# A linear-attention layer gated by an FP4 network: x1 is transposed by DMA in 16-bit halves in 23 of 32 blocks, and the first layer norm's gain and shift move to VectorE

## The chip, the core and the metric

The kernel runs on one core of a Trainium2 chip. The time is the device time of one execution in microseconds (us); each figure is a median of several runs. Engines are named as in the profile: PE is TensorE's matmul, PEld its weight load, DVE is VectorE, ACT is ScalarE, POOL is GpSimd, SP is SyncE, whose queue issues nearly all DMAs.

## What is computed

The input `x` is 4 x 2048 x 256 in float32. It is normalised once, and two branches use the result:

```python
xn = layernorm(x)                                   # no gain, no shift
# branch 1: linear attention with 16 heads of 64, then a feed-forward network
Q = elu(xn @ Wq + bq) + 1;  K = elu(xn @ Wk + bk) + 1;  v = xn @ Wv + bv
KV = einsum("bshd,bshm->bhdm", K, v)
Z = 1 / (einsum("bshd,bhd->bsh", Q, K.sum(1)) + 1e-6)
o = einsum("bshd,bhdm,bsh->bshm", Q, KV, Z)
x1 = layernorm(xn + o @ Wo + bo) * g1 + be1
s = layernorm(x1 + gelu(x1 @ W1 + b1) @ W2 + b2) * g2 + be2
# branch 2: a gated network on FP4-rounded activations and weights
g = silu(fp4_linear(silu(fp4_linear(xn, w_gate)) * fp4_linear(xn, w_up), w_down))
out = x + s * g
```

The change concerns the line of `x1`, and how its result reaches the product with `W1`, which needs it transposed.

## The kernel before

A batch has 2048 tokens and is cut into eight blocks of 256, so there are 32 blocks, n = 0 to 31. A block lies on chip as 128 partitions of two tokens (index `j`) by 256 features.

A prologue prepares the weights and sums the keys of the first batch. Then the loop over n runs the query side of block n: Q, the attention product, the first layer norm, the feed-forward network and the FP4 network, spread in a software pipeline over neighbouring iterations. In the first three batches the same iterations also work off the keys of the next batch ("subs", two per block): in the first four blocks of a batch's turn the keys' inputs are normalised and transposed (`f == 0`), in the last four they are loaded back from memory for the other half of the heads. The last batch, blocks 24 to 31, has no keys beside it.

All of TensorE's instructions keep the order in which the program writes them (`mm` and `tr`, lines 102 to 106; the profile gives their lines as L103 and L106). For the other engines and for SP's queue a planner orders the instructions ahead of time, by the program's order and by what it expects to be ready; `tc.issue_after(ins)` puts instructions behind a given one on its engine. Once ordered, each engine takes its list strictly in turn and waits at the head of it.

Around the change an iteration n runs thus (lines 1221 to 1285):

- `attention_norm(n)` (line 951): mean and variance of x1 on VectorE, the power -1/2 on GpSimd (line 430), then two `tensor_scalar` on VectorE give (x1 - mean) * rstd. Gain and shift are not applied here.
- `keys_in` for the next two subs; then on TensorE `ffn_2(n - 1, 20)`, the first 20 products of the second feed-forward matrix of the block before (`py`).
- `scales_h`, `scales_x`: VectorE finds the FP4 scales of the next blocks.
- `x1_T(n)` (line 956): four PE transposes of x1 into PSUM (`pt_x`), and two ScalarE activations that take them out into `x1T`, with g1 as scale and be1 as bias, each a column per feature.
- `keys_apart` (line 502) for both next subs. Where the keys' input was just normalised, it is transposed by DMA: ScalarE copies the upper and the lower 16-bit halves of the floats apart, one transposing DMA on SP moves both, and later `keys_T` (line 523) joins the halves by one ScalarE copy.
- `spread_scales`: a PE transpose of the scales (`pscale`), a store, and eight loads that spread them into `qT`.
- `ffn_2(n - 1, 28)`, then `q_of(n + 1)`: 32 matmul instructions (`pq`) in four PSUM tiles; each tile takes an exponential on ScalarE (`e`) and one VectorE instruction (`zq`).
- `grid_of_h`, `grid_T`, `grid_of_x` (FP4 rounding and its transposing DMAs), `output(n - 1)`, `keys_T` of the first next sub, and `ffn_1(n)` (line 968): 32 matmul instructions (`pf`) that read `x1T`, and gelu.

The joining copy of the second sub follows in the next iteration, behind the exponential of the first sub's keys. The tokens' own x1, wanted again in `output`, gets its gain and its shift on GpSimd in `ffn_addend` (line 811): times g1, plus a row `shift` that holds be1 + b2 (folded once by `add_b2`, line 267).

Buffers that matter: `mm_tile`, four PSUM banks in a ring for most products; tag `e` (three tiles: the exponentials of Q and of keys, and the keys' separated halves), tag `kk` (three: K's tiles and the transposed halves), and tag `zs` (one tile of three parts: sums that the attention product of the first three batches reads).

Of the kernel before, what the change touches and what calls it, by code (L numbers as in the profile page):

```python
# [8 lines left out]
F32 = mybir.dt.float32  # L9
# [13 lines left out]
def linear_attention_gated_by_fp4_ffn(  # L23
# [81 lines left out]
    def tr(*args, **kw):  # L105
        return tc.keep_in_program_order(nc.tensor.transpose(*args, **kw))  # L106
# [75 lines left out]
    for _ in range(24):  # L182
# [13 lines left out]
    W2_OF = {"11": 0, "21": 1, "22": 2, "t1": 3, "t2": 4, "t3": 5, "t4": 6}  # L196
    row_tiles = {
        name: const.tile([P, 1, D], F32, name=f"{name}_r")
        for name in ("bo", "g1", "shift", "g2", "be2")
    }  # L200
    rows = {name: t.to_broadcast([P, TB, D]) for name, t in row_tiles.items()}

# [3 lines left out]
    def load_row(name, v, dep):  # L206
        load_when(dep, row_tiles[name][:, 0, :], as_rows(v))
# [10 lines left out]
    def w2_sums():  # L218
# [20 lines left out]
            lambda dep: wv_bias(1),  # L239
            lambda dep: load_wv(0, dep),  # L240
            lambda dep: load_row("g1", g1, dep),
            lambda dep: load_row("shift", be1, dep),
            lambda dep: load_row("g2", g2, dep),
            lambda dep: load_row("be2", be2, dep),
        ],
# [18 lines left out]

    cols = {}

    def add_b2(dep):
        b2_r = work.tile([P, D], F32, tag="s", name="b2_r", bufs=1)
        load_when(dep, b2_r, as_rows(b2))
        shift = row_tiles["shift"][:, 0, :]  # L270
        nc.gpsimd.tensor_tensor(shift, shift, b2_r, ALU.add)

    def small_constants():


        vs = (("b1", b1), ("g1", g1), ("be1", be1))
        n = sum(v.shape[0] // P for _, v in vs)
        brow = work.tile([n, P], F32, tag="z", name="brow", bufs=1)
        r = 0
        for name, v in vs:  # L280
            k = v.shape[0] // P
            nc.sync.dma_start(brow[r : r + k, :], v.rearrange("(c p) -> c p", p=P))
            cols[name] = (r, r + k)
            r += k
        yield
        pb = mm_tile("pb")
        tr(pb[:, :n], brow, ident[:n, :n])
        bcol = const.tile([P, n], F32, name="bcol")
        vector.tensor_copy(bcol, pb[:, :n])
        for name, (lo, hi) in cols.items():  # L290
            cols[name] = bcol[:, lo:hi]
        yield


# [2 lines left out]
    def fp4_scale(x, am, name):  # L297

        nb = x.shape[1]
        rs = small.tile([P, I // BLK], F32, tag="rs", name=f"rs_{name}")[:, :nb]  # L300
        vector.tensor_reduce(am, x, AX.X, ALU.max, apply_absolute_value=True)
        vector.tensor_scalar(am, am, -1.0 / 6.0, -1e-12, ALU.mult, ALU.min)
        vector.reciprocal(rs, am)
        return rs
# [146 lines left out]

    xn_d, xnT_d = {}, {}
    keys = {}

# [42 lines left out]
            nc.sync.dma_start(xn, xn_d[n])  # L499
            nc.sync.dma_start(xnT, xnT_d[n])  # L500

    def keys_apart(b, sub, issue=None):
# [7 lines left out]
        half = keys[b, sub][0].bitcast(U16).rearrange("p j (c f h) -> p h c j f", c=ND, h=2)  # L510
        apart = work.tile([P, 2, ND, TB, P], U16, tag="e", name=f"apart_{n}", bufs=3)
        with tc.issue_after(issue) if issue is not None else nullcontext():
            for h in range(2):
                scalar.copy(apart[:, h], half[:, h])
        apartT = work.tile([P, 2, ND * T], U16, tag="kk", name=f"apartT_{n}", bufs=3)
        nc.sync.dma_start(
            apartT.rearrange("p h (m t) -> p (h m) t", t=P),
            apart.rearrange("p h c j f -> p (h c j f)"),
            transpose=True,
        )  # L520
        keys[b, sub].append(apartT)

    def keys_T(b, sub, issue=None):

        f, bi = divmod(sub, NB)
        if f > 0:
            return
        n = b * NB + bi
        xn, *apartT = keys[b, sub]
        xnT = work.tile([P, ND, T], F32, tag="xnT_k", name=f"xnT_k_0_{n}", bufs=3)  # L530
        if apartT:
            with tc.issue_after(issue):
                scalar.copy(
                    xnT.bitcast(U16).rearrange("p c (t h) -> p h (c t)", h=2), apartT[0]
                )
# [275 lines left out]
    def ffn_addend(n, behind=True):  # L811

        x1 = blk[n]["x1"]
        with tc.issue_after(pool["last"]) if behind else nullcontext():
            nc.gpsimd.tensor_tensor(x1, x1, rows["g1"], ALU.mult)
            pool["last"] = nc.gpsimd.tensor_tensor(x1, x1, rows["shift"], ALU.add).ins


    def q_of(n, chunks=range(NH)):
# [131 lines left out]
    def attention_norm(n):  # L951
        x1 = blk[n]["x1"]
        mv, rstd = stats(x1, f"1_{n}")
        normalize(x1, x1, mv, rstd)

    def x1_T(n):
        x1 = blk[n]["x1"]
        pt = transposes(x1, f"x1_{n}")
        x1T = work.tile([P, ND, T], F32, tag="x1T", name=f"x1T_{n}", bufs=1)
        for c in range(ND):  # L960
            ins = scalar.activation(
                x1T[:, c, :], pt[:, c, :], AF.Identity,
                bias=cols["be1"][:, c : c + 1], scale=cols["g1"][:, c : c + 1],
            )
        blk[n]["x1T"] = x1T
        blk[n]["act"] = ins.ins

    def ffn_1(n, chunks=range(NF)):
        x1T = blk[n]["x1T"]
# [80 lines left out]
    for n in range(NB):  # L1050
# [47 lines left out]
        ready = weight  # L1098
        if n == 4:
            w_down_sb = load_down()  # L1100
        if n == 5:
            add_b2(dep)
        if n == 6:
            load_xn(0)
            scales_x(0)
# [49 lines left out]
    for n in range(NBLK):  # L1155
# [80 lines left out]
        if more[0]:  # L1236
            scales_h(n + 1, 0)
            with tc.issue_after(qz_ins) if not subs else nullcontext():
                scales_h(n + 1, 1)
            if more[1]:  # L1240
                scales_x(n + 2)
        for sub in next_subs if n == 0 else ():
            keys_in(bn + 1, sub)
        x1_T(n)
        if not subs:
            ffn_addend(n, False)
        if n == last:
            gate_addend(n)
        for sub in next_subs:
            keys_apart(bn + 1, sub, blk[n]["act"])  # L1250

        if n > 0 and not subs:
            ffn_2(n - 1, 26)
# [2 lines left out]
        if n > 0:  # L1256
            ffn_2(n - 1, 28)
        if more[0]:
            q_of(n + 1)
        if more[0]:  # L1260
            grid_of_h(n + 1, 0)
            grid_T(n + 1, 0, NI)
# [9 lines left out]
            step(m_half)  # L1272
        for sub in next_subs[:1]:
            keys_T(bn + 1, sub, blk[n + 1]["exp"])
        if n + 1 == last:
            ffn_1(n, range(2))
            sums(last)
            ffn_1(n, range(2, NF))
            gpsimd_behind(blk[n]["hT"][:, NF - 1, :])
            gate_addend(n)  # L1280

            w2_last = wk_sb.rearrange("p c (e d) -> p (c e) d", d=D)
            nc.sync.dma_start(w2_last, by_chunks(W2))
        else:
            ffn_1(n)
# [46 lines left out]
```

## Time and profile before

| | us |
|---|---|
| median of 3 runs (1883.41 to 1885.26) | 1884.52 |
| the profiled execution | 1883.6 |
| its span on the core | 1881.8 |
| PE busy in it | 1860.8 |
| DVE busy in it | 1381.8 |
| ACT busy in it | 706.5 |
| POOL busy in it | 382.5 |

The span is the time between the first and the last instruction that the profiler saw; the execution's time also holds what lies around it. The rows of the instruction groups that the change touches, by the groups view (count, us busy in all, mean ns of one):

| engine, group | count | us | ns |
|---|---|---|---|
| PE, transposes of x1 (`pt_x`) | 128 | 21.5 | 282 |
| ACT, x1T out of PSUM, 128 x 256 | 64 | 32.6 | 560 |
| DVE, normalising x1, 128 x 256 | 64 | 23.5 | 410 |
| POOL, x1 times g1, 128 x 512 | 32 | 40.5 | 1266 |
| POOL, x1 plus shift, 128 x 512 | 32 | 41.4 | 1293 |
| ACT, keys' halves apart, 128 x 512 of 16 bits | 44 | 24.9 | 616 |
| ACT, keys' halves joined, 128 x 1024 of 16 bits | 22 | 29.4 | 1336 |

Matmul instructions overlap, so the sum of their durations is more than the time they take up: in the chain of waits the four transposes of a block take 0.44 us. How to read it: PE is busy in 99% of the span, and the 40 slices show a granted clock of full speed throughout. The other engines have free time, but within an iteration it is unevenly spread, so what matters for them is whether TensorE comes to wait for what they deliver.

### The profile page before, as it was taken

How to read it: one execution, taken by the hardware profiler on the slowest of the kernel's cores; microseconds unless marked ns; L12 is line 12 of the kernel's file. 1: busy time of each engine (PE TensorE's matmuls, PEld its weight loads, DVE VectorE, ACT ScalarE, POOL GpSimd, SP SyncE). 2: the span in 40 equal slices, each digit the busy share in tenths (PEclk: the TensorE clock that was granted, in tenths of full speed). 3: DMA queues.
4: the chain of work that ended last, by engine and by line, in shares of the span. 5: the costliest groups of instructions: out<-in, count | busy, mean ns of one | idle time of the engine just before them, and what ended most of it. 6: DMA issues, size and time to landing. Idle time of an engine off the chain costs nothing.

```text
span 1881.8 us, 25202 instructions
## 1 busy us (share of the span) xinstructions
PE 1860.8 (99%) x9324; PEld 1382.2 (73%) x9324; DVE 1381.8 (73%) x2524; ACT 706.5 (38%) x1190; POOL 382.5 (20%) x363
## 2 busy tenths in 40 slices
PE   8999999999999999999999999999999999999998
PEld 4456677777777777777777787777777788888887
DVE  5676677766677877777677787776776777888875
ACT  2343544324334335443233543353323333333332
POOL 1411322011122212220112221222101122222212
PEclk9999999999999999999999999999999999999999
DMA  5525655444535456635344654564443444444542
GB/s 182 194 77 127 116 120 102 100 102 94 96 63 99 111 98 122 143 66 110 81 89 79 119 100 104 94 139 90 91 88 71 104 77 83 89 83 84 92 83 50
DMA packets 229433, 188.77 MB, mean 100 GB/s; under 512 B 107687, under 2 KB 191155, under 8 KB 229310
## 3 DMA queue, kind: packets, MB, share of 16 engines
q1 hardware_dynamic: 228476, 185.58, 47.4%
q8 instruction: 74, 1.21, 0.3%
q10 hardware_dynamic: 834, 1.58, 0.3%
q14 instruction: 49, 0.40, 0.1%
HBM read 131.96 MB, written 32.59 MB: 87 GB/s over the span
## 4 chain that ended last, share of the span: by engine, by line
PE 77%; DVE 10%; DMA 9%; SPq 1%; issue 1%; POOL 1%; ACT 1%; POOLq 0%; DVEq 0%; ACTq 0%
PE pg L103 14%; PE pk L103 10%; PE pxk L103 10%; PE pf L103 9%; PE pa L103 8%; PE pq L103 8%; PE pd L103 7%; PE py L103 7%; DMA zb<-z_d 2%; DMA qT<-scale_d 2%; PE pz L103 1%; DMA xn_d<-xn_k 1%; DMA z_d<-z 1%; DVE x L119 1%; POOL rstd L430 1%
## 5 line engine op out<-in xcount | busy, mean ns | idle before, releaser
L430 POOL TENSOR_TENSOR rstd<-rstd,neg_half 128x2 f32<-128x2 f32 (+1 forms) x97 | 77.3, 797 | 1324.8 <-DVE rstd L119 964.9
L103 PE MATMUL pg<-wgu,qT 128*128 128x352 f32 x1024 | 308.5, 459 | 0.2 <-PE pm L103 0.2
L103 PEld LDWEIGHTS pg<-wgu,qT 128*128 128x128 f32 x1024 | 194.3, 190 | 113.8 <-issue 11.5
L103 PE MATMUL pk<-wk_sb,xnT_k 128*128 128x512 f32 x512 | 230.4, 592 | 1.2 <-ACT xnT_k L119 1.2
L103 PE MATMUL pf<-x1T,w_sb 128*128 128x256 f32 x1024 | 227.7, 380 | 2.2 <-DVE zq L119 1.6
L103 PE MATMUL pxk<-kk,xn_k 128*128 128x512 f32 x496 | 227.9, 598 | 1.1 <-DVE kk L119 1.1
L103 PE MATMUL pq<-xnT,wq_sb 128*128 128x256 f32 x1024 | 227.6, 380 | 0.9 <-DVE zq L119 0.8
L103 PEld LDWEIGHTS pf<-x1T,w_sb 128*128 128x128 f32 x1024 | 193.6, 190 | 32.3 <-DVE zq L119 6.0
L103 PEld LDWEIGHTS pq<-xnT,wq_sb 128*128 128x128 f32 x1024 | 191.8, 190 | 27.1 <-DVE zq L119 2.4
L119 DVE SCALAR_TENSOR_TENSOR kk<-ek,pk 128x512 f32<-128x512 f32 x128 | 85.5, 684 | 170.3 <-ACT ek L119 170.3
L103 PE MATMUL pd<-wd,qT 128*128 128x256 f32 x768 | 172.9, 380 | 1.1 <-DVE qT L119 1.1
L119 ACT ACT_TABLE_LOAD x121 | 155.2, 1283 | 49.2 <-PE pk L103 34.3
L103 PEld LDWEIGHTS pk<-wk_sb,xnT_k 128*128 128x128 f32 x512 | 97.0, 190 | 102.6 <-issue 90.3
L119 ACT ACTIVATE x1T<-pt_x,bcol 128x256 f32<-128x256 f32 x64 | 32.6, 560 | 357.8 <-PE pt_x L106 357.8
L103 PEld LDWEIGHTS pd<-wd,qT 128*128 128x128 f32 x768 | 145.3, 190 | 27.9 <-DVE qT L119 4.4
L103 PEld LDWEIGHTS pxk<-kk,xn_k 128*128 128x128 f32 x496 | 89.4, 190 | 99.2 <-issue 87.0
L119 DVE TENSOR_TENSOR h<-h,pg 128x352 f32<-128x352 f32 x128 | 66.0, 516 | 105.4 <-PE pg L103 103.2
L119 ACT ACTIVATE h<-pg 128x352 f32<-128x352 f32 x128 | 58.8, 459 | 211.3 <-PE pg L103 211.2
L119 ACT ACTIVATE hT<-pf,bcol 128x256 f32<-128x256 f32 x256 | 105.7, 471 | 66.0 <-PE pf L103 65.6
L119 DVE TENSOR_TENSOR zq<-zq,zb 128x1024 f32<-128x1024 f32 x64 | 79.2, 1238 | 64.9 <-DMA zb<-z_d 64.5
L103 PE MATMUL py<-w_sb,hs 128*128 128x128 f32 x992 | 122.0, 275 | 0.0
L119 ACT ACTIVATE e<-pq,neg_one 128x512 f32<-128x512 f32 x128 | 86.6, 685 | 84.7 <-PE pq L103 70.6
(159 smaller groups left out, 2789.4 us busy)
## 6 DMA issues: line engine op xcount, KB each, us to landing
zb<-z_d SPq DMA_DIRECT2D x128, 256.0 KB, 6.3
qT<-scale_d SPq DMA_DIRECT2D x248, 128.0 KB, 6.0
x_k<-in_L_attn_src_dram SPq DMA_DIRECT2D x32, 256.0 KB, 4.0
x<-in_L_attn_src_dram SPq DMA_DIRECT2D x32, 256.0 KB, 2.9
xn_d<-xn_k SPq DMA_DIRECT2D x32, 256.0 KB, 2.7
xn<-xn_d SPq DMA_DIRECT2D x32, 256.0 KB, 2.7
xnT_d<-xnT_k SPq DMA_DIRECT2D x32, 256.0 KB, 2.0
xnT<-xnT_d SPq DMA_DIRECT2D x32, 256.0 KB, 4.0
```

Of the source, the lines that this page charges most:

```text
L103: return tc.keep_in_program_order(nc.tensor.matmul(*args, **kw))
L119: ins = op(*args, **kw)
L430: pool["last"] = nc.gpsimd.tensor_tensor(rstd[:, j0:j1], rstd[:, j0:j1], neg_half[:, j0:j1], ALU.pow).ins
```

## The change

In blocks 1 to 23, `x1_T` no longer uses TensorE. ScalarE copies x1's 16-bit halves apart into one part of a `zs` tile, one transposing DMA writes them to a second part, and ScalarE joins them into `x1T` behind the exponentials of the first half of the next block's Q. Blocks 0 and 24 to 31 keep the PE transposes, with one plain ScalarE copy out of PSUM in place of the two activations.

Gain and shift are applied before the transposition: `attention_norm` computes (x1 - mean) * g1 and then (...) * rstd + be1, by four `scalar_tensor_tensor` on VectorE in place of two `tensor_scalar`. GpSimd's `ffn_addend` only adds b2.

The first of the next two subs has its halves separated into the third part of the `zs` tile instead of an `e` tile; the second sub's separation moves from ahead of Q to behind the first sub's joining copy. Small things: `b2` gets a row of its own, `shift` and `add_b2` go, the columns of g1 and be1 go, the FP4 reciprocals use three buffers instead of four, and in block 0 `x1_T` stands ahead of `keys_in`.

```diff
+    def apart(x, xp, xpT):
+        half = x.bitcast(U16).rearrange("p j (c f h) -> p h c j f", c=ND, h=2)
+        for h in range(2):
+            ins = scalar.copy(xp[:, h], half[:, h])
+        nc.sync.dma_start(
+            xpT.rearrange("p h (m t) -> p (h m) t", t=P),
+            xp.rearrange("p h c j f -> p (h c j f)"),
+            transpose=True,
+        )
+        return ins.ins
+
+    def together(xT, xpT, issue):
+        with tc.issue_after(issue):
+            scalar.copy(xT.bitcast(U16).rearrange("p c (t h) -> p h (c t)", h=2), xpT)
...
-            nc.gpsimd.tensor_tensor(x1, x1, rows["g1"], ALU.mult)
-            pool["last"] = nc.gpsimd.tensor_tensor(x1, x1, rows["shift"], ALU.add).ins
+            pool["last"] = nc.gpsimd.tensor_tensor(x1, x1, rows["b2"], ALU.add).ins
...
     def attention_norm(n):
         x1 = blk[n]["x1"]
         mv, rstd = stats(x1, f"1_{n}")
-        normalize(x1, x1, mv, rstd)
+        for j in range(TB):
+            vector.scalar_tensor_tensor(
+                x1[:, j, :], x1[:, j, :], mv[:, j, 0:1], rows["g1"][:, j, :], ALU.subtract, ALU.mult
+            )
+        for j in range(TB):
+            vector.scalar_tensor_tensor(
+                x1[:, j, :], x1[:, j, :], rstd[:, j : j + 1], rows["be1"][:, j, :], ALU.mult, ALU.add
+            )
+
+    def x1_by_dma(n):
+        return n > 0 and in_seven(n // NB)
 
     def x1_T(n):
         x1 = blk[n]["x1"]
-        pt = transposes(x1, f"x1_{n}")
-        x1T = work.tile([P, ND, T], F32, tag="x1T", name=f"x1T_{n}", bufs=1)
-        for c in range(ND):
-            ins = scalar.activation(
-                x1T[:, c, :], pt[:, c, :], AF.Identity,
-                bias=cols["be1"][:, c : c + 1], scale=cols["g1"][:, c : c + 1],
-            )
-        blk[n]["x1T"] = x1T
-        blk[n]["act"] = ins.ins
+        x1T = blk[n]["x1T"] = work.tile([P, ND, T], F32, tag="x1T", name=f"x1T_{n}", bufs=1)
+        if x1_by_dma(n):
+            t = work.tile([P, 3, ND * T], F32, tag="zs", name=f"apart_x1_{n}", bufs=1).bitcast(U16)
+            xp, blk[n]["room"] = (
+                t[:, i].rearrange("p (h c j f) -> p h c j f", h=2, c=ND, j=TB) for i in (0, 2)
+            )
+            blk[n]["apart"] = t[:, 1].rearrange("p (h t) -> p h t", h=2)
+            blk[n]["act"] = apart(x1, xp, blk[n]["apart"])
+        else:
+            blk[n]["act"] = scalar.copy(x1T, transposes(x1, f"x1_{n}")).ins
+
+    def x1_together(n, issue):
+        if x1_by_dma(n):
+            together(blk[n]["x1T"], blk[n].pop("apart"), issue)
...
+        x1_T(n)
         for sub in next_subs if n == 0 else ():
             keys_in(bn + 1, sub)
-        x1_T(n)
...
-        for sub in next_subs:
-            keys_apart(bn + 1, sub, blk[n]["act"])
+        room = blk[n].pop("room", None)
+        for sub in next_subs[:1]:
+            keys_apart(bn + 1, sub, blk[n]["act"], room)
...
         if more[0]:
-            q_of(n + 1)
+            q_of(n + 1, range(NH // 2))
+            x1_together(n, blk[n + 1]["exp"])
+            q_of(n + 1, range(NH // 2, NH))
...
         for sub in next_subs[:1]:
             keys_T(bn + 1, sub, blk[n + 1]["exp"])
+        for sub in next_subs[1:]:
+            keys_apart(bn + 1, sub, blk[n + 1]["exp"])
```

More of the change, by code (lines that the diff above doesn't have):

```diff
@@ L198, in linear_attention_gated_by_fp4_ffn @@
         name: const.tile([P, 1, D], F32, name=f"{name}_r")
-        for name in ("bo", "g1", "shift", "g2", "be2")
+        for name in ("bo", "g1", "be1", "b2", "g2", "be2")
     }
@@ L241, in linear_attention_gated_by_fp4_ffn @@
             lambda dep: load_row("g1", g1, dep),
-            lambda dep: load_row("shift", be1, dep),
+            lambda dep: load_row("be1", be1, dep),
+            lambda dep: load_row("b2", b2, dep),
             lambda dep: load_row("g2", g2, dep),
@@ L265, in linear_attention_gated_by_fp4_ffn @@
     cols = {}
[L267 to L271, printed above, removed]
-    def small_constants():
[L276 to L284, printed above, removed]
+    def small_constants():
+        brow = work.tile([NF, P], F32, tag="z", name="brow", bufs=1)
+        nc.sync.dma_start(brow, b1.rearrange("(c p) -> c p", p=P))
         yield
         pb = mm_tile("pb")
[L287 to L291, printed above, removed]
+        tr(pb[:, :NF], brow, ident[:NF, :NF])
+        cols["b1"] = const.tile([P, NF], F32, name="bcol")
+        vector.tensor_copy(cols["b1"], pb[:, :NF])
         yield
@@ L299, in fp4_scale @@
         nb = x.shape[1]
-        rs = small.tile([P, I // BLK], F32, tag="rs", name=f"rs_{name}")[:, :nb]
+        rs = small.tile([P, I // BLK], F32, tag="rs", name=f"rs_{name}", bufs=3)[:, :nb]
         vector.tensor_reduce(am, x, AX.X, ALU.max, apply_absolute_value=True)
@@ L500, in keys_in, with keys_apart @@
             nc.sync.dma_start(xnT, xnT_d[n])
-    def keys_apart(b, sub, issue=None):
+    def keys_apart(b, sub, issue=None, xp=None):
         f, bi = divmod(sub, NB)
@@ L509, in keys_apart @@
         n = b * NB + bi
-        half = keys[b, sub][0].bitcast(U16).rearrange("p j (c f h) -> p h c j f", c=ND, h=2)
-        apart = work.tile([P, 2, ND, TB, P], U16, tag="e", name=f"apart_{n}", bufs=3)
+        if xp is None:
+            xp = work.tile([P, 2, ND, TB, P], U16, tag="e", name=f"apart_{n}", bufs=3)
+        apartT = work.tile([P, 2, ND * T], U16, tag="kk", name=f"apartT_{n}", bufs=3)
         with tc.issue_after(issue) if issue is not None else nullcontext():
[L513 to L519, printed above, removed]
-        )
+            apart(keys[b, sub][0], xp, apartT)
         keys[b, sub].append(apartT)
@@ L531, in keys_T @@
         if apartT:
[L532 to L535, printed above, removed]
+            together(xnT, apartT[0], issue)
         else:
@@ L1100, in linear_attention_gated_by_fp4_ffn @@
             w_down_sb = load_down()
-        if n == 5:
-            add_b2(dep)
         if n == 6:
@@ L1248, in linear_attention_gated_by_fp4_ffn @@
             gate_addend(n)
-        for sub in next_subs:
-            keys_apart(bn + 1, sub, blk[n]["act"])
+        room = blk[n].pop("room", None)
+        for sub in next_subs[:1]:
+            keys_apart(bn + 1, sub, blk[n]["act"], room)
+        room = None
         if n > 0 and not subs:
```

## The prediction

> **What bounds the kernel now.** I read the page's busy shares first, then the windows between the x1 transposes of neighbouring blocks, then the chain of waits, then the timeline. Blocks are numbered n = 0 to 31 by the order of their x1 transposes.
>
> ```profile
> PE 1860.8 (99%) x9324; PEld 1382.2 (73%) x9324; DVE 1381.8 (73%) x2524; ACT 706.5 (38%) x1190; POOL 382.5 (20%) x363
> 1398.48:1454.93 56.45, 56.45 (x288) 42.27 (x286) 40.00 (x73) 19.57 (x33) 9.23 (x8) 1.00 0.42 79
> 1602.15:1646.52 44.37, 44.00 (x231) 35.95 (x230) 36.67 (x62) 15.57 (x26) 9.92 (x8) 1.00 0.47 88
> ```
>
> The last two are windows of one block: length, then busy PE, PEld, DVE, ACT, POOL, granted clock, DMA share. Block 21 is TensorE without a hole at a full clock; blocks of the last batch have 0.37 us of holes. So an edit pays by what it takes from TensorE's own list, or by a hole that it closes; work elsewhere costs only where TensorE comes to wait. The chain of waits (start, length, what) gives TensorE's list for blocks 20 and 21:
>
> ```profile
> 1340.57 0.71 POOL rstd L430
> 1341.28 0.03 issue
> 1341.30 0.42 DVE x L119
> 1341.72 0.04 issue
> 1341.77 0.87 PE pt_x L106 x4
> 1342.64 0.11 PE pscale L106
> 1342.75 1.79 PE py L103 x16
> 1344.53 6.91 PE pq L103 x32
> 1351.44 6.91 PE pf L103 x32
> ...
> 1398.65 0.44 PE pt_x L106 x4
> 1399.08 0.11 PE pscale L106
> ```
>
> The four x1 transposes take 0.44 us where x1 is ready and 0.87 us where they wait in their midst for VectorE. Between them and the first user of their result, pf, lie pscale, py and pq: 0.11 + 1.79 + 6.91 = 8.81 us. That is the room the DMA path gets.
>
> **The change part by part.**
>
> *Transposes leave TensorE* in blocks 1 to 23. Undisturbed they take 1399.08 - 1398.65 = 0.43 to 0.44 us: 23 x 0.436 = **-10.0 us**. Nothing hides them today, so all of it counts.
>
> *Waits for x1 leave with them.* In blocks 5, 6, 12, 13 and 20 the transposes stretch over 0.69 to 0.87 us (about 0.26 too much, 1.3 together), and in blocks 12, 13 and 20 they also begin late: in block 12 at 881.28, where the py x16 before them began at 879.16 and gives way after 1.79 us as in the chain above, so 0.33 late; 0.30 and 0.57 in the other two. Together **-2.5 us**. Late next is pscale, whose input is ready over 3 us before it in these blocks, so nothing takes their place.
>
> *The new path must land inside the 8.81 us.* Where no keys are normalised (blocks 3 to 6, 11 to 14, 19 to 23) x1 comes latest, so I take block 12, from the timeline:
>
> ```profile
> 880.07 0.70 POOL L430 TENSOR_TENSOR rstd<-rstd,neg_half 128x2 f32<-128x2 f32 x1 [39.61 <-DVE rstd L119]
> 880.81 0.73 DVE L119 TENSOR_SCALAR x<-x,mv,rstd 128x256 f32<-128x256 f32 x2 [0.81 <-POOL rstd L430]
> 887.60 0.69 ACT L119 ACTIVATE e<-pq,neg_one 128x512 f32<-128x512 f32 x1 [1.10 <-PE pq L103]
> 890.99 0.69 ACT L119 ACTIVATE e<-pq,neg_one 128x512 f32<-128x512 f32 x1 [0.98 <-PE pq L103]
> ```
>
> x1 is normed at 881.54. The new norm is two pairs of SCALAR_TENSOR_TENSOR, priced by s<-s,mv,g of the same shape (492 ns; two, 0.40 apart, span 0.88). The first pair doesn't need rstd and falls into the 0.81 us that VectorE waits for POOL's power; so x1 is done at about 880.0 + 2 x 0.88 = 881.8, 0.25 later. The keys' own path prices the rest:
>
> ```profile
> L119 ACT COPY apart<-xn_k x44: 600/616/636, 196.2 to 1229.7; 128x512 uint16<-128x512 uint16 x44
> DMA to landing us min/median/max: 3.4/3.9/4.5
> L119 ACT COPY xnT_k<-apartT x22: 1324/1332/1363, 203.6 to 1245.0; 128x1024 uint16<-128x1024 uint16 x22
> ```
>
> The two copies span 1.14 us: issue at 883.0, landing at 886.9 (887.5 at worst). Without transposes and wait pq starts at 883.0, so the second exponential of Q, behind which the joining copy is ordered, ends about 887.2; the copy runs to 888.6, and pf wants x1T at 889.9. **Slack 1.3 us, cost nothing**; uncovered, it is paid in full, per block. Behind the joining copy on ScalarE stand two exponentials of Q (0.69 us each) and VectorE's zq behind them; TensorE needs those banks only inside pf, 1.7 us and more later. In the other blocks x1 is ready some 2 us earlier.
>
> *A rule against this.* The Trainium skill, "VectorE: DVE Perf Modes", section "Rules for kernel authors", sends a 128x128 transpose to TensorE wherever PSUM will do as its target, and the table in "The three transpose paths" gives the DMA 1309 ns for one 16 bit 128x128. x1 is eight of those: by the table 10.5 us, landing at 893.5, pf about 5 us late, 4.5 lost per block, some 1990 us in all. The row above is the same eight squares in 3.4 to 4.5 us. I take the row: same queue, form and size. It lets the transfer fit, and then slow is free.
>
> *SP's queue.* Each x1 adds one issue of about 1.24 us. Behind it stand scale_d and its eight loads into qT. In block 12 these are issued at 883.57 and from 885.11 to 888.74; with 6.0 us to landing and a slip of 0.7 to 1.3 us they are in by 896, and the first product with qT comes after 900. Nothing.
>
> *ScalarE* loses two x1T evictions (1.02 us), gains 1.14 + 1.33. Of the two keys blocks' halves, the second (1.12 us of copies and a wait for its store) moves from ahead of Q's exponentials to behind the first block's joining copy, ahead of gelu. There ScalarE waits for pf 0.38 and 0.89 us in block 9, which absorbs it. The second transfer then lands some 5 us before its joining copy in the next block. Its bank of the e ring also comes free: "ACT e <- DMA apartT" (3.1 us in all) goes.
>
> *VectorE* gains 2 x 0.88 - 0.73 = 1.0 us per block, 0.35 to 0.8 of it inside an idle stretch. Where keys are normalised (blocks 1, 2, 7 to 10, 15 to 18) the list is dense:
>
> ```profile
> 308.44 0.19 ACT L119 COPY xn_k<-ones 128x2 f32<-128x2 f32 x1 [1.06 <-DMA xn_d<-xn_k]
> 308.54 0.26 ACT L119 COPY scaleT<-pscale 128x128 f32<-128x128 f32 x1
> 314.07 1.99 PE L103 MATMUL pq<-xnT,wq_sb 128*128 128x256 f32 x8 [0.67 <-DVE zq L119]
> ```
>
> These are block 2: TensorE already waits 0.67 us for zq. Such holes sum to 2.6 us over the ten blocks. Against the added 0.7 us or so stands that Q's first exponential no longer comes behind the second block's copies. Bounds -2.6 (holes close) to +8 (0.8 in each of ten); I take 0, since both shifts are near 1 us.
>
> *Norm with PE transposes still there* (blocks 0 and 24 to 31): x1 is just in time today (transposes begin within 0.1 us of its end), so the 0.21 to 0.25 us show: 9 x 0.22 = **+2.0**. GpSimd's lost multiplication (1.27 us) frees VectorE there: y<-xn,rs_x took 1.43 us beside it in block 25 against 0.83 on average, ahead of qT, whose product pd waits 0.18 us a block. I take **-0.7** back (0 to -1.4).
>
> *b2 unfolded, columns of g1 and be1 gone, one buffer of rs fewer*: one DMA more or less in the prologue, three scale tiles alive at once in three buffers; 0 within 0.3 us.
>
> **Sum.** -10.0 - 2.5 + 2.0 - 0.7 = **-11.2 us**. The profiled execution took 1883.6 (span 1881.8), so 1872.4; the median of the runs, 1884.5, is 0.9 higher, so I forecast **1873.3**, own range 1869 to 1879.
>
> **Rivals.**
>
> *A, x1 comes late (slower).* Place: ScalarE's joining copy. If it is ordered behind Q's last exponential or its transfer is late, pf waits. In block 12 that exponential ends at 891.68, 0.89 after pf's start; with 1.33 of copy and a step pf is 2.27 late, 1.83 net of the transposes, x 23 = +42, less 2.5 and 0.7 and plus 2.0 as above: about **1925**. It decides from a landing over 5.5 us after issue. For it: ScalarE's order is planned ahead and fixed, and a mistaken order makes ready work stand. Against: in block 2 the planner put a copy that had to wait 1.06 us for a store ahead of a scaleT that was ready, so it takes transfers for faster than they are, which puts the joining copy early; and 22 of 22 landings took 4.5 us or less. Only some blocks late gives 1886 to 1900.
>
> *B, VectorE takes the gain.* 0.8 us more in each of ten key blocks: 1873.3 + 8 = **1881**. For it the hole of block 2; against it the earlier exponential.
>
> *C, the key blocks' holes close as well*: 1873.3 - 2.6 = **1870.7**. For it the same earlier exponential.
>
> **Chances.** Forecast 0.63, A 0.22 (a quarter of it in the milder form), B 0.10, C 0.05. I set the range 1868 to 1890: it takes in B and C and the mildest of A, leaving out some 0.18. What a measurement of this kernel tells from no change is about 0.2%, 3.8 us: faster is the forecast, C and a bit of B, 0.69; within it most of B, 0.09; slower A, 0.22.
>
> **What would show it.** In the chain of blocks 3 to 6 the list should run py, pscale, py, pq, pf without pt_x, 56.0 us a block; the transposing DMA of x1 should land within 4.5 us, its joining copy stand between the second and third exponential, and pf have no idle before it. Blocks 24 to 30 should be 44.4 to 44.7 us long. The forecast is wrong if pf waits for ScalarE's joining copy, if the copy stands behind the fourth exponential, or if pq in blocks 7 to 10 waits over 0.5 us for zq.

## The result, and the profile after

| | us |
|---|---|
| before, median of 6 runs (1883.41 to 1885.26) | 1884.18 |
| after, median of 6 runs (1891.7 to 1895.67) | 1894.02 |
| ratio, with its 95% interval | 1.0053 (1.0042 to 1.0064) |
| forecast | 1873.3 |
| the profiled executions: before, after | 1883.6, 1895.58 |

The change makes the kernel about 10 us slower, where 11 us less were forecast: an error of some 21 us. From the page of after, the span, the busy time of each engine, and the shares of the chain of waits:

```profile
span 1893.6 us, 25087 instructions
PE 1856.6 (98%) x9232; PEld 1372.2 (72%) x9232; DVE 1387.3 (73%) x2588; ACT 732.5 (39%) x1204; POOL 345.3 (18%) x330
PE 54%; DVE 20%; DMA 12%; issue 7%; POOL 3%; ACT 2%; SPq 2%; POOLq 0%; DVEq 0%; ACTq 0%
```

TensorE has 92 instructions fewer, the 23 x 4 transposes, yet the span is 11.8 us longer. VectorE gained only 5.5 us of busy time, which at 73% looks harmless. The third row is the warning: before, the chain was 77% PE and 10% DVE; now VectorE has 20% of it. The windows of block 21 and of a block in the last batch, here from one transposition of the scales to the next (length, then busy PE, PEld, DVE, ACT, POOL, clock, DMA share, GB/s):

```profile
1407.33:1465.13 57.80, 56.51 (x284) 41.66 (x283) 40.96 (x76) 20.92 (x34) 8.15 (x7) 1.00 0.41 81
1615.54:1659.89 44.35, 44.02 (x230) 36.10 (x231) 36.61 (x63) 15.16 (x25) 8.84 (x7) 1.00 0.48 88
```

Block 21 had no hole before (56.45 of 56.45). Now 1.29 us of TensorE stand empty, three times what the transposes took; the block of the last batch is as long as it was. The chain of waits of after for the same iteration (start, length, what; it comes here from GpSimd):

```profile
1419.14 1.48 DVE o L119
1420.62 0.61 DVE zq L119
1421.27 3.72 PE pf L103 x16
```

Before, pscale, py, pq and pf followed each other here on TensorE alone. Now the chain reaches pf through VectorE: the second layer norm's output `o`, then the last `zq`. The waits view of after says where TensorE stands (engine, group, line, released by: us in all, times, longest):

```profile
PE pq L103 <- DVE zq L119: 10.2, 9, 2.5
PE pq L103 <- DVE s L119: 8.0, 9, 1.3
```

`s` is written by the additions with which `output(n - 1)` adds the feed-forward result `py` to x1. Before, the first row held 0.8 us and the second didn't exist. To place all of it I took the starts of TensorE's groups from the timeline and set each stretch (say from pq to pf) against the shortest of its kind in any profiled run; the excess is waiting. The parts, after against before:

| part of the span | before | after | difference |
|---|---|---|---|
| up to the scales of iteration 0 | 192.6 | 193.4 | +0.8 |
| iterations 0 to 22 | 1319.2 | 1329.2 | +10.0 |
| of it: the 23 sets of transposes, undisturbed | 10.0 | 0 | -10.0 |
| of it: waits at the transposes and behind `pa` | 4.5 | 0 | -4.5 |
| of it: waits from pq to pf (Q) | 3.7 | 24.9 | +21.2 |
| of it: waits from pf to pk (in pf itself, or ahead of the keys' product) | 1.2 | 4.0 | +2.8 |
| iterations 23 to 29 | 314.1 | 315.2 | +1.1 |
| the rest | 55.9 | 55.9 | 0 |

So the expected gain arrived, 14.5 us of it, and Q took 21 us back. Of the 24.9 us, 14.4 fall in the ten iterations where keys are normalised (1, 2, 7 to 10, 15 to 18) and 10.4 in the others, where VectorE had room. The parts leave 0.5 us of the +10.0 unplaced.

Block 12 shows how a block with room comes to wait. From the timeline of after (start, length, engine, instruction, idle time before it and what ended it; in this and the other timelines, rows that don't bear on the point are left out):

```profile
883.99 0.88 DVE L119 SCALAR_TENSOR_TENSOR x<-x,rstd,be_r 128x256 f32<-128x256 f32 x2 [0.60 <-POOL rstd L416]
886.12 1.24 SPq L446 DMA_TRANSPOSE apart_x<-apart_x  x1
886.91 0.89 DVE L119 SCALAR_TENSOR_TENSOR h<-m_h,h 128x704 f32<-128x704 bf16 x1 [1.44 <-ACT m_h L119]
888.23 0.69 ACT L119 ACTIVATE e<-pq,neg_one 128x512 f32<-128x512 f32 x1 [0.68 <-PE pq L103]
889.80 0.68 DVE L119 TENSOR_TENSOR s<-x,py 128x512 f32<-128x512 f32 x1
890.51 2.12 DVE L119 TENSOR_TENSOR s<-s,py 128x384 f32<-128x384 f32 x4
890.61 1.32 ACT L119 COPY x1T<-apart_x 128x1024 uint16<-128x1024 uint16 x1
892.55 0.68 DVE L119 SCALAR_TENSOR_TENSOR zq<-e,pq 128x512 f32<-128x512 f32 x1
892.78 1.97 PE L103 MATMUL pq<-xnT,wq_sb 128*128 128x256 f32 x8 [1.13 <-DVE s L119]
```

The additions that came early, the first exponential and the first `zq` in the timeline of before:

```profile
881.46 0.68 DVE L119 TENSOR_TENSOR s<-x,py 128x512 f32<-128x512 f32 x1
882.17 0.55 DVE L119 TENSOR_TENSOR s<-s,py 128x384 f32<-128x384 f32 x1
884.08 0.56 DVE L119 TENSOR_TENSOR s<-s,py 128x384 f32<-128x384 f32 x1 [1.35 <-PE py L103]
885.81 0.69 ACT L119 ACTIVATE e<-pq,neg_one 128x512 f32<-128x512 f32 x1 [1.05 <-PE pq L103]
886.76 0.68 DVE L119 SCALAR_TENSOR_TENSOR zq<-e,pq 128x512 f32<-128x512 f32 x1
```

(`h`, `y`, ScalarE's `m_h` and `m_x`, and `grid` are steps of the FP4 rounding.) Before, the first `zq` started 0.26 us after its exponential ended (885.81 + 0.69 = 886.50). Three of the five additions were done by then, in time that VectorE had to spare, and two came behind it. After, all five stand ahead of it in VectorE's list, directly before it, and so do two roundings of x: the exponential ends at 888.92, `zq` starts at 892.55, 3.6 us later, and VectorE is busy all that time. Earlier it had been idle for 1.44 us, up to 886.91, waiting for `m_h`, with the additions behind that wait; the first two of them were done at this point in before. Such idle time at the head of a fixed list is what no busy share can show. Q's fourth tile needs a PSUM bank that VectorE gives back, and waits; by its row the wait ended with the last addition (890.51 + 2.12 = 892.63), and `zq` was still later.

x1's own path is fine here: its transposing DMA is issued at 886.12, the joining copy ends at 891.93, and pf would have been due at 886.30 + 6.91 = 893.21 without Q's wait. From the views of the tiles `apart_x` and `x` of after (durations as min/median/max in ns; the landings are those of every transfer from the tile, x1's and the keys'):

```profile
L119 ACT COPY x1T<-apart_x x23: 1321/1328/1338, 254.9 to 1528.8; 128x1024 uint16<-128x1024 uint16 x23
DMA to landing us min/median/max: 2.7/2.8/5.6
```

```profile
L119 DVE SCALAR_TENSOR_TENSOR x<-x,mv,g_r x64: 446/472/482, 190.6 to 1870.2; 128x256 f32<-128x256 f32 x64
L119 DVE SCALAR_TENSOR_TENSOR x<-x,rstd,be_r x64: 476/482/486, 192.1 to 1871.6; 128x256 f32<-128x256 f32 x64
```

The trace holds a landing for only some of the transfers: five of x1's 23, at 2.7 to 4.0 us, and two of the keys' from this tile, of which one is the 5.6.

### The profile page after: what moved, and what is told of

Read it like the earlier page. It is cut to its first block, busy times and chain, and to the rows that moved or that the text cites. A ratio compares the mean times of both kernels' runs of the same rounds, so it can differ in the third digit from the quotient of the medians.

```text
span 1893.6 us, 25087 instructions
## 1 busy us (share of the span) xinstructions
PE 1856.6 (98%) x9232; PEld 1372.2 (72%) x9232; DVE 1387.3 (73%) x2588; ACT 732.5 (39%) x1204; POOL 345.3 (18%) x330
## 4 chain that ended last, share of the span: by engine, by line
PE 54%; DVE 20%; DMA 12%; issue 7%; POOL 3%; ACT 2%; SPq 2%; POOLq 0%; DVEq 0%; ACTq 0%
PE pg L103 10%; PE pf L103 9%; PE pk L103 8%; PE pxk L103 7%; PE pq L103 5%; PE pd L103 5%; DMA zb<-z_d 5%; PE pa L103 5%; POOL rstd L416 3%; DMA xn<-xn_d 3%; DMA z_d<-z 3%; DVE x L119 3%; PE py L103 2%; DVE hs L119 2%; DVE zq L119 2%
## 5 line engine op out<-in xcount | busy, mean ns | idle before, releaser
L416 POOL TENSOR_TENSOR rstd<-rstd,neg_half 128x2 f32<-128x2 f32 (+1 forms) x97 | 84.2, 868 | 1370.7 <-DVE rstd L119 1305.6
L103 PE MATMUL pq<-xnT,wq_sb 128*128 128x256 f32 x1024 | 232.6, 382 | 18.4 <-DVE zq L119 10.2
L103 PEld LDWEIGHTS pq<-xnT,wq_sb 128*128 128x128 f32 x1024 | 191.2, 191 | 49.8 <-DVE zq L119 14.4
L103 PEld LDWEIGHTS py<-w_sb,hs 128*128 128x128 f32 x992 | 116.6, 192 | 0.0
```

The lines of the kernel that those rows point to most:

```text
L103: return tc.keep_in_program_order(nc.tensor.matmul(*args, **kw))
L416: pool["last"] = nc.gpsimd.tensor_tensor(rstd[:, j0:j1], rstd[:, j0:j1], neg_half[:, j0:j1], ALU.pow).ins
```

## The experiments

Two suspects: VectorE's extra work in the norm, and the order of VectorE's list. In the table every ratio is to the kernel before, measured beside it; waits are those of iterations 0 to 22 in one profiled execution. e1 and e5 leave g1 and be1 out altogether, GpSimd's multiplication by g1 too.

| run | median us | before | ratio (95% interval) | waits at Q | pf to pk |
|---|---|---|---|---|---|
| e1: after, norm as before | 1886.12 | 1882.2 | 1.0020 (1.0011 to 1.0029) | 13.3 | 12.0 |
| e2: new norm only | 1890.5 | 1882.2 | 1.0041 (1.0026 to 1.0056) | 11.9 | 0.2 |
| e3: after, additions behind first zq | 1878.0 | 1882.2 | 0.9978 (0.9969 to 0.9988) | 8.6 | 0.4 |
| e4: before, additions behind first zq | 1886.53 | 1882.2 | 1.0025 (1.0015 to 1.0036) | 7.7 | 1.0 |
| e5: e3, norm as before | 1864.36 | 1880.47 | 0.9908 (0.9893 to 0.9922) | 0.2 | 0 |
| e6: e3, second separation early | 1889.0 | 1880.47 | 1.0045 (1.0029 to 1.0062) | 17.7 | 0.3 |
| e7: e3, m_x behind first exponential | 1872.41 | 1880.47 | 0.9956 (0.9941 to 0.9971) | 4.0 | 0.6 |
| e8: e7, first separation late | 1910.31 | 1880.47 | 1.0155 (1.0140 to 1.0170) | 1.1 | 32.4 |
| e9: e5 made whole, g1 and be1 in W1 and b1 | 1876.79 | 1880.42 | 0.9979 (0.9970 to 0.9988) | 0.6 | 0.3 |
| e10: after again | 1890.14 | 1880.42 | 1.0051 (1.0034 to 1.0067) | 21.6 | 3.7 |
| e11: e9, folded later | 1872.39 | 1881.69 | 0.9956 (0.9941 to 0.9971) | 0.5 | 0.3 |
| e12: e9, m_x behind first exponential | 1875.69 | 1881.69 | 0.9971 (0.9958 to 0.9983) | 0.3 | 0.3 |

The waits of one kernel differ between executions: after shows 24.9 us at Q in one and 21.6 (e10) in the other. The profiled executions of e3 (1875.29 us) and e6 (1884.4) were the fastest of their kernels, so their waits are on the low side.

### One part at a time: the norm, and the path

e1 keeps the DMA path and takes the new norm out; e2 keeps the norm and takes the path out.

```diff
     def attention_norm(n):                      # e1
-        for j in range(TB):
-            vector.scalar_tensor_tensor(...)
-        for j in range(TB):
-            vector.scalar_tensor_tensor(...)
+        normalize(x1, x1, mv, rstd)
```

> The changed kernel with the first layer norm as it was: two tensor_scalar on VectorE; g1 and be1 are left out of x1 altogether, b2 is still added by GpSimd. It has the x1 transfer by DMA, but not VectorE's added 1.0 us per block. Theory V (VectorE's added work makes zq late): the waits of TensorE at the fourth tile of Q go back to the 2.6 us of before, time about 1872. Theory O (the order that the planner now writes for VectorE, with the five output additions ahead of the first zq, makes it late, whoever does the norm): the order of VectorE's list in blocks 3 to 6, 11 to 14, 19 to 23 is still the late one, so most of the 24 us of waits stay, time 1884 to 1892.

```diff
     def x1_by_dma(n):                           # e2
-        return n > 0 and in_seven(n // NB)
+        return False
...
-        for sub in next_subs[:1]:
+        for sub in next_subs:
             keys_apart(bn + 1, sub, blk[n]["act"], room)
...
-        for sub in next_subs[1:]:
-            keys_apart(bn + 1, sub, blk[n + 1]["exp"])
```

> The changed kernel without the transfer: x1 is transposed on TensorE in all blocks and both keys' separations stand ahead of Q again; only the norm with g1 and be1 on VectorE and GpSimd's single addition remain. Theory V: VectorE is as loaded as in the changed kernel, so TensorE waits at Q as there, 1890 to 1905 (24 us of waits, 10 us of transposes). Theory O: in the blocks without keys to normalise the first zq stands ahead of three of the five additions again, so the waits at Q are a few us in all, plus 0.25 us per block for the later x1: 1886 to 1892.

e1 is still slower than before though VectorE does no more than it did, and e2 is slower by 0.41% with TensorE's list as it was. So each of the two parts costs on its own. In the thirteen blocks without keys to normalise, e1's five additions stand ahead of the first `zq` as in after; in e2, with the transposes on TensorE, two do (three in before), and the other three follow it. It is the path that moved them, not the norm. In the ten blocks with keys three stand ahead in after, e1 and e2, and four or five in before. Why the planner does so (x1 no longer makes TensorE's list wait, so `py` is expected earlier against Q) is my reading; its prices aren't visible in a trace.

About half of e1's 12.0 us from pf to pk are pf itself waiting, also for `zq`, by the waits view:

```profile
PE pf L103 <- DVE zq L119: 6.5, 10, 0.7
```

### The order put back

e3 ties the additions of the block before behind the first `zq` in blocks 1 to 23, and changes nothing else of after. e4 makes the same edit in the kernel before.

```diff
-            vector.scalar_tensor_tensor(zq[:, cc : cc + 2, :], e, 1.0, pq, ALU.min, ALU.max)
+            blk[n]["zq_ins", cc] = vector.scalar_tensor_tensor(
+                zq[:, cc : cc + 2, :], e, 1.0, pq, ALU.min, ALU.max
+            ).ins
...
-            output(n - 1)
+            with tc.issue_after(blk[n + 1]["zq_ins", 0]) if x1_by_dma(n) else nullcontext():
+                output(n - 1)
```

> The changed kernel with one edit: in blocks 1 to 23 the output additions of the block before are ordered behind the first zq of Q on VectorE. The work of every engine is the same. Theory O: the fourth tile of Q finds its bank about 3 us earlier, the waits at Q fall from 24 us to under 6, time 1872 to 1878. Theory V: VectorE has no more time than before, something else of it comes late by the same amount, time 1888 or more.

> Control: the kernel before with the same edit of the order (blocks 0 to 23). Theory O: it has only 2.6 us of waits at Q, so 1881.5 to 1885; if it gained as much as the edit gains on the changed kernel, the order would be an independent improvement and not the cause of the loss.

e3 takes 0.75% off after, from 1.0053 to 0.9978, and no wait at Q over 0.05 us is left in iterations 3 to 6, 11 to 14 and 19 to 22. e4 is slower than before: the edit is no improvement by itself, it mends what the path displaced. What is left in e3, 8.6 us, lies where keys are normalised, but for 0.3 us in iteration 0. The timeline of e3 in block 7:

```profile
590.29 0.88 DVE L119 SCALAR_TENSOR_TENSOR h<-m_h,h 128x704 f32<-128x704 bf16 x1
590.41 5.35 PE L103 MATMUL pq<-xnT,wq_sb 128*128 128x256 f32 x24
591.75 0.73 DVE L119 TENSOR_SCALAR xn_k<-x_k,mv,rstd 128x256 f32<-128x256 f32 x2 [0.58 <-POOL rstd L416]
592.40 0.89 DVE L119 SCALAR_TENSOR_TENSOR grid<-m_h,h 128x704 bf16<-128x704 bf16 x1
593.21 0.69 DVE L119 SCALAR_TENSOR_TENSOR y<-xn,rs_x 128x512 f32<-128x512 f32 x1
593.99 0.63 ACT L119 ACTIVATE m_x<-y 128x512 bf16<-128x512 f32 x1 [4.40 <-DVE y L119]
594.73 1.14 ACT L119 COPY apart_x<-xn_k 128x512 uint16<-128x512 uint16 x2
595.78 1.26 ACT L119 ACTIVATE e<-pq,neg_one 128x512 f32<-128x512 f32 x2
597.23 1.99 PE L103 MATMUL pq<-xnT,wq_sb 128*128 128x256 f32 x8 [1.47 <-DVE zq L119]
```

ScalarE stands idle for 4.40 us, though Q's first products are done before that idle time is over, because `m_x` is ahead of the exponential and VectorE's `y` is late; then the keys' halves follow, and the exponential, and `zq`. TensorE's row names `zq`, but `zq` waited for `e`, `e` stood behind `m_x`, and `m_x` waited for `y`. A wait is to be followed back until an engine is reached that was truly busy. Here it is VectorE; what kept it busy shows against the next experiment.

### Both parts out

e5 is e3 with the norm of e1.

> The third experiment's kernel (additions behind the first zq) with the first layer norm as it was; g1 and be1 are left out of x1. It prices VectorE's added 1.0 us per block where the order is mended. Theory V: those 8.6 us of waits that are left at Q, all in the ten blocks that normalise keys, are VectorE's added work, so they fall under 3 us and the time is about 6 us below the third experiment's. Theory O: they are not its length but what stands ahead of Q's first exponential on ScalarE (the separation of keys and the rounding copy m_x, which wait for VectorE), so at least half of them stays.

The timeline of e5 in the same block 7:

```profile
587.43 0.69 DVE L119 SCALAR_TENSOR_TENSOR y<-xn,rs_x 128x512 f32<-128x512 f32 x1
588.38 7.07 PE L103 MATMUL pq<-xnT,wq_sb 128*128 128x256 f32 x32
589.36 0.88 DVE L119 SCALAR_TENSOR_TENSOR h<-m_h,h 128x704 f32<-128x704 bf16 x1
590.49 0.68 ACT L119 ACTIVATE e<-pq,neg_one 128x512 f32<-128x512 f32 x1
590.76 0.89 DVE L119 SCALAR_TENSOR_TENSOR grid<-m_h,h 128x704 bf16<-128x704 bf16 x1
```

In e5 `y` starts 0.95 us ahead of Q's first product, in e3 2.80 us behind it. The norm's own work is 1.0 us of that. The rest is order again: in e3 `h`, its rounding `grid` and two more of the keys' normalisations stand ahead of `y`, in e5 they stand behind it. The timelines show the same in all ten blocks with keys: `y` is late in after, e3, e6 and e7 and early in before, e1, e2 and e5. So the planner moves it only where both parts are in. On the mean of the ten it starts 2.5 us ahead of Q in before, 1.4 ahead in e2 (the norm's own work alone), 2.0 ahead in e5, and 2.3 behind in e3. A version with the new norm and `y` tied ahead of `h` was not run, so what the extra work alone costs where both orders are mended stays open.

The four corners: with the additions early, the new norm costs 1.0053 - 1.0020 = 0.33% (6 us); with them behind the first `zq`, 0.9978 - 0.9908 = 0.70% (13 us), the late `y` included. The additions' order costs 1.12% (21 us) with the norm as before and 0.75% (14 us) with the new one. They overlap, since late additions and a late `y` make Q wait for the same VectorE. With neither, the kernel is 0.92% (17 us) faster than before. Not all of that is the path's, since e5 also leaves out GpSimd's multiplication: iterations 0 to 22 are 17.1 us shorter (1302.1 for 1319.2), iterations 23 to 29, which have no DMA path, 2.8. The 0.70% between e3 and e5 is partly in these last iterations too: they sum to 314.7 us in e3 and 311.3 in e5; the other 8.4 us are the waits at Q.

### ScalarE's list

e6 puts the second sub's separation ahead of Q again, as before; e7 moves `m_x`; e8 moves the first separation too.

```diff
-                grid_of_x(n + 2, blk[n]["act"])                  # e7, e8
+                grid_of_x(n + 2, blk[n + 1]["exp", 0] if x1_by_dma(n) else blk[n]["act"])
...
             x1_together(n, blk[n + 1]["exp"])                    # e8 only; gone from ahead of Q
+            for sub in next_subs[:1]:
+                keys_apart(bn + 1, sub, blk[n + 1]["exp"], room)
```

> The third experiment's kernel, with the second keys block's separation back ahead of Q, as before the change. If that move (the prediction's relief of ScalarE, 1.1 us per block that normalises keys) is worth what was said, the waits at Q grow by up to 1 us in each of ten blocks, so 4 to 10 us slower than the third experiment; if the first exponential is late for other reasons, no difference beyond 2 us.

> The third experiment's kernel, with the rounding copy m_x of the block after next ordered behind Q's first exponential on ScalarE (blocks 1 to 23). In the block before the ninth, ScalarE stood 4.4 us at m_x for VectorE's y, with Q's first product done 3.6 us before its exponential. Theory O: the exponential no longer waits for y, and the waits at Q fall from 8.6 to 5 us or less, 3 to 6 us faster than the third experiment. Theory V: no gain.

> As the run before, and the first keys block's separation also stands behind Q's first half, after x1's joining copy. Theory O: all waits at Q but 2 us go, 1868 to 1873, unless the keys' joining copy, which must end before the next block's keys product, comes late now and TensorE waits there (pf to pk), up to 2 us in each of ten blocks, which would give 1875 to 1890.

e6 loses 0.67% against e3, so moving the second separation is a real relief: waits at Q go from 8.6 to 17.7 us, 7 us of it in the ten blocks with keys and 2 in iteration 0. e7 halves what e3 had left. e8 empties Q of waits as well, but overshoots. In its waits view:

```profile
PE pk L103 <- ACT xnT_k L119: 29.9, 12, 4.2
```

and, for the keys' product of block 8, a row of the windows view:

```profile
678.72:684.05 5.33, 5.33 (x9) 2.03 (x9) 0.69 (x1) 1.93 (x2) 0.03 (x1) 0.68 0.65 189
```

In block 8 of e8 the keys' transposing DMA is issued at 669.69, 9.2 us behind the start of Q (5.1 in e7), and its joining copy starts only at 677.33; the keys' product was due at 674.52, when pf ends, and starts at 678.72. Behind that hole of 4.2 us the granted clock is 0.68, and the product takes 5.33 us (3.52 in e7, at a clock of 1.00); over iterations 0 to 22 such slow products add 9.6 us to the waits. That makes e8 slower than even its pessimistic expectation of 1875 to 1890 us. So the separation has its place ahead of Q after all: what comes of it is wanted 14 us behind the start of Q.

### The extra work taken off VectorE without leaving it out

e5 leaves g1 and be1 out. e9 computes everything: it multiplies the rows of W1 by g1 once in the prologue, and adds the product of W1 and be1 to b1; the tokens' own x1 gets its g1 and be1 + b2 on GpSimd, as before.

```diff
+    def fold_w1():
+        pbe = mm_tile("pbe")
+        for c in range(NF):
+            for d in range(ND):
+                mm(pbe[:, c : c + 1], w1_sb[:, d, c * P : (c + 1) * P], cols["be1"][:, d : d + 1], ...)
+        vector.tensor_tensor(cols["b1"], cols["b1"], pbe[:, :NF], ALU.add)
+        for d in range(ND):
+            g = cols["g1"][:, d : d + 1].to_broadcast([P, FF])
+            nc.gpsimd.tensor_tensor(w1_sb[:, d, :], w1_sb[:, d, :], g, ALU.mult)
...
+            nc.gpsimd.tensor_tensor(x1, x1, rows["g1"], ALU.mult)
```

> The fifth experiment made whole: x1 by DMA, additions behind the first zq, the norm by two tensor_scalar, and g1 and be1 put into W1 and b1 once in the prologue (W1's rows times g1, b1 plus W1 times be1) for the transposed x1; for the tokens' own x1 GpSimd multiplies by g1 and adds be1 + b2 as in the kernel before. Both theories as they now stand: VectorE has before's work in a mended order, so TensorE has no waits at Q. The fifth experiment's ratio 0.991, plus 1 to 4 us for the prologue and GpSimd's multiplication beside VectorE: 1864 to 1870 where the kernel before takes 1880.5 to 1884.5. If it is above 1875, GpSimd's second pass over x1 costs more than VectorE's own.

> The changed kernel once more, on the chip of the run above, so that all four cells (order late or mended, norm plain or with gain and shift) and the whole version stand against the same kernel before: ratio 1.004 to 1.0065.

e10 repeats after beside e9 and gives the first ratio again. e9 takes 1876.79 us where 1864 to 1870 were expected. The reading set down for a time above 1875, that GpSimd's second pass costs more than VectorE's own work, does not hold in iterations 0 to 22: e9's iterations 0 to 22 are as short as e5's (1301.0 against 1302.1 us), but its span is 10.9 us longer. Of that 8.3 us are lost ahead of iteration 0 (8.6 by the next). From e9's timeline:

```profile
112.43 3.63 PE L103 MATMUL pbe<-bcol,w_sb 128*128 128x1 f32 x32
115.92 3.79 POOL L300 TENSOR_TENSOR w_sb<-w_sb,bcol 128x1024 f32<-128x1024 f32 x2 [3.28 <-PE pbe L103]
116.09 0.16 DVE L119 TENSOR_TENSOR bcol<-bcol,pbe 128x8 f32<-128x8 f32 x1 [2.99 <-PE pbe L103]
117.88 1.87 DVE L119 TENSOR_SCALAR scale<-scale 128x32 f32<-128x32 f32 x1
119.80 0.48 PE L106 MATMUL pscale_-1_848<-ident,scale 128*128 128x128 f32 x1 [3.74 <-DVE scale L119]
```

and from its windows, the twelve keys' products behind it:

```profile
120.07:127.44 7.37, 7.37 (x13) 3.12 (x13) 4.09 (x7) 2.35 (x5) 1.27 (x1) 0.70 0.28 76
```

Three things add up. The 32 small products take 3.63 us. Then TensorE waits 3.74 us for scales that stand behind the addition to b1 in VectorE's list: the fixed list again, but `scale<-scale` also takes 1.87 us here, while GpSimd multiplies W1, and 0.18 in e5. And the granted clock falls to 0.70, so that the twelve keys' products take 7.37 us where e5's take 5.16 at 1.00. e11 calls `fold_w1` after the first gate steps, 21 us later; e12 adds e7's edit to e9.

> The kernel of e9 (first products of Q ordered ahead of the output additions; g1 and be1 folded into W1 and b1), with the folding moved some 30 us later in the prologue: behind the scales and the grid of block 0 and the first gate steps, ahead of block 0's scales of h. Nothing is left out. Theory: of the 8.6 us that e9 loses against e5 ahead of block 1, the 3.7 us in which TensorE waited for the scales of block 0 came from VectorE's place behind the 32 small matmuls; later in the prologue nothing of TensorE waits for VectorE in that stretch, so the wait goes and the matmuls' 3.6 us stay: about 1873 us, ratio 0.996, no wait of TensorE over 1 us near the folding. Rival: the loss is GpSimd's (its two multiplications of W1, 3.8 us, and the row's addition stand ahead of what the prologue needs of it), or VectorE waits for the fold at its new place for something just as urgent: then the time stays at 1877 us or rises, ratio 0.998 or more.

> The kernel of e9 with one more order edit, that of e7: ScalarE's m_x of the next block (grid_of_x) stands behind Q's first exponential in blocks 1 to 23. Nothing is left out. Theory: with the norm plain again VectorE's y is early enough, e9 has only 0.6 us of waits at Q left, so there is nothing for this edit to gain: within 0.1% of e9, 1876 to 1878 us, ratio 0.998. Rival: m_x still holds up exponentials in some blocks in ways that the sum of waits doesn't show; then 2 to 4 us less, ratio 0.996.

In e11 no wait stands at the folding any more. The small products and the 16 products of `pg` behind them, in the view of windows:

```profile
133.37:138.03 4.66, 4.66 (x34) 4.66 (x33) 0.13 (x1) 1.85 (x5) 0.20 (x1) 0.74 0.03 1
138.03:145.10 7.07, 7.07 (x17) 4.09 (x17) 6.41 (x11) 1.72 (x3) 3.72 (x3) 0.69 0.02 0
```

The granted clock is 1.00 up to the folding and falls during it, though TensorE has no hole there. The small products take 4.66 us and `pg` 7.07 (4.83 in e5): together 6.9 of the 7.0 us by which e11 reaches iteration 0 later than e5. Why the clock falls there was not tested. The span is 1.5 us shorter than e9's, the median 4.4, with intervals of the ratios that just overlap. Block 21 of e11, in the view of windows:

```profile
1389.12:1445.13 56.01, 56.01 (x283) 41.83 (x282) 40.71 (x74) 20.77 (x34) 9.25 (x8) 1.00 0.41 84
```

TensorE has no hole, and the block is 56.0 us long, as predicted for the change. e12 is within 0.1% of e9: with `y` in time, `m_x` no longer holds anything up. Against e5 the last batch keeps 4.8 us (316.1 against 311.3). There GpSimd's second pass over x1 runs beside VectorE. The group of `y`, in the last batch, of e9 and then of after (count, busy us, mean ns):

```profile
L119 DVE SCALAR_TENSOR_TENSOR y<-xn,rs_x 128x512 f32<-128x512 f32 x4 | 5.7, 1435 | 0.1
```

```profile
L119 DVE SCALAR_TENSOR_TENSOR y<-xn,rs_x 128x512 f32<-128x512 f32 x5 | 3.4, 679 | 0.0
```

The instruction is the same. In e9, as in before (1432 ns), GpSimd's second pass is running when it starts; in after and e5 (691 ns) there is no second pass, and it takes half the time. That accounts for 0.75 us a block of VectorE time; that it makes all of the 4.8 us wasn't tested.

e7 and e11 are both 0.44% faster than the kernel before. The two were not joined in a version with one GpSimd pass and no extra work on VectorE.

## Why the prediction was wrong

**The step that failed** is VectorE's: "Bounds -2.6 (holes close) to +8 (0.8 in each of ten); I take 0, since both shifts are near 1 us." Measured, the waits at Q grew by 21.2 us and those between pf and pk by 2.8. The step took VectorE's list as in the trace of before, with four instructions exchanged, and priced durations. I had asked of ScalarE's list whether a planner would put a ready instruction behind one that waits (rival A), but not of VectorE's, and there it did so twice.

First, a term that wasn't there. In the thirteen blocks that I had counted as free, the output additions moved to directly ahead of Q's first `zq`: 10.4 us of waits. Putting them behind it was worth 14 us with the new norm and 21 with the old, in both kinds of blocks together (e3, e5).

Second, the term itself, in the ten blocks with keys. With the additions mended (e3), waits at Q are 8.6 us against 3.7 before: the netted shifts cost 4.9, inside my bounds but not 0. I had set an earlier exponential against the norm's work. It is there with the norm as before: in the ten blocks Q's first exponential ends on the mean 2.8 us behind the start of Q in e5, and 4.7 in before. With the new norm it is back at 4.7 (e3; 4.9 in after), since it stands behind `m_x`, `m_x` waits for `y`, and `y` came late by the norm's 1.0 us and by some 3 us of changed order. A shift on one engine can't be netted against a shift on another that waits for the first. The new norm without the path (e2) raised the waits at Q by 8.2 us, 1.5 of it in iteration 0; that is without the relief of the moved separation.

That the two orders make Q wait is shown by e3 (the additions) and by e5 and e7 (`y` and `m_x`); how the waits behind `y` divide between the norm's length and the changed order is not.

**What held, by the prediction's own steps:**

- *Transposes leave TensorE*, -10.0: shown. With the order mended and the norm as before, the gain is there (e5).
- *Waits for x1*, -2.5: 2.9 went at the transposes, and 1.6 more behind `pa`.
- *The new path inside the room*: x1's five recorded landings took 2.7 to 4.0 us, where 3.4 to 4.5 were taken. (Those, called 22 of 22, rest on the six of 22 for which the trace of before holds a landing.) In block 12 the copy ended 1.28 us ahead of when pf would have been due; 1.3 was worked out, though by the rows shown there the second exponential would have ended at 887.4 and not 887.2, which makes it 1.1. The joining copy stands between the second and the third exponential, as expected, and pf doesn't wait for it. Rival A fell. The row from the trace was right against the estimate of 10.5 us for eight squares, which multiplies the Trainium skill's figure for one ("VectorE: DVE Perf Modes", section "The three transpose paths").
- *SP's queue*: no wait of TensorE traced back to it.
- *ScalarE*, second separation as a relief: right in sign, and larger than I gave it credit for, 0.67% (e6 against e3).
- *Norm with PE transposes, and GpSimd's relief*, +2.0 and -0.7: together +1.3; measured +0.8 ahead of iteration 0 and +1.1 behind iteration 22. Each alone was bigger. With the norm as before and one GpSimd pass (e5) iterations 23 to 29 sum to 311.3 us against 314.1 before, a relief of 2.8; the new norm then takes 3.4 (e3) to 3.9 (after) of it back.
- *Rival B* had the right engine and the wrong size: 0.8 us in each of ten blocks. It saw the cost of instructions, not of their order. *Rival C* is what e5 shows at Q, with the norm as before: the holes close, to 0.2 us.

Of the signs named beforehand, two came out against the forecast: blocks 3 to 6 took 59.7, 56.2, 57.4 and 57.2 us, not 56.0 (the first of each four is longer in every version, 58.8 in e11), and TensorE waited 2.2, 1.7 and 1.8 us at Q in iterations 7, 8 and 10. Iterations 24 to 29 took 44.1 to 44.4 us, a little less than forecast, but for one of 45.1.

## What to carry to other kernels

Where engines take fixed lists that a planner orders, taking an instruction off the bounding engine also reorders the others. So before pricing a change by durations, ask which short instructions, once delayed, stop the bound (here the additions and the first `zq`, which give PSUM banks back, and `y`, which Q's exponential comes to wait for), and what may be put ahead of them; tie that order down in the same change. Don't net a delay on one engine against an advance on another that waits for the first. When a wait shows, follow it past the name in the row, through each engine that stood idle, to one that was busy.

## What was not expected of the hardware

- x1's transposing DMA landed in 2.7 to 4.0 us (five recorded) where the keys' own, of the same form and size, took 3.9 at the median before (six recorded) and 4.5 after (nine). Why x1's are faster, and whether x1's slow the keys' down, was not tested.
- `scalar_tensor_tensor` with a row as third operand took 472 to 482 ns where `tensor_scalar` on the same 128 x 256 took 410; the norm's four cost 1.91 us instead of 0.82 by their own durations.
- The one VectorE instruction `y<-xn,rs_x` takes 679 ns or 1435 ns; in the long case a GpSimd pass over x1 is running when it starts.
- The granted clock fell to 0.68 behind a hole of 4.2 us (block 8 of e8) and, the only time within the loop of after, to 0.57 behind its longest hole at Q (2.5 us, iteration 16); behind one of 3.3 us in e8 it stayed at 1.00. It fell to 0.74 and 0.69 during and behind 32 small products without a hole (e11). What decides was not tested.
- Q's fourth tile waited now for the output additions (block 12 of after), now for a `zq` (block 7 of e3). That fits a bank that is handed to whichever tile gives one back first; which bank it is no view shows.
